# A graph-network stack on one core: layer 2's polynomial at half width, and layer 0's turned adjacency of four groups made for all graphs at once through device memory

## The chip, the cores and the metric

The kernel runs on one core of a Trainium2 chip. Time is the device time in microseconds (us); three runs of the kernel before gave 2142.8, 2142.81 and 2144.53 us, a median of 2142.81 us. The profile is of one further execution.

The engines are called by their names in the profile: PE is TensorE (matmul), PEld its weight loads, DVE is VectorE, ACT is ScalarE, POOL is GpSimd and SP is SyncE, which here only issues transfers (DMAs). "L825" is line 825 of the kernel before.

## What is computed

128 graphs of 64 nodes with 256 features pass through four layers, each followed by a residual addition and a layer norm. All arithmetic is in float32.

```python
# layer 0: five groups of nodes (25, 9, 7, 6 and 6 of the first 25), two graph convolutions each
A = adj[:, idx][:, :, idx] + eye;  deg = A.sum(-1);  dinv = where(deg == 0, 0, deg ** -0.5)
h   = relu((dinv[:, :, None] * A * dinv[:, None, :]) @ (x_g @ W1[g]) + b1[g])
out = relu((same normalized A) @ (h @ W2[g]) + b2[g]);   fused[:, idx] += softmax(fusion_w)[g] * out
# layer 1: one convolution with (adj + eye), normalized in the same way, over all 64 nodes
# layer 2: P = adj / (row_sum + 1e-9);  out = leaky((c0 + c1 P + c2 P^2 + c3 P^3) (x W^T) + b)
# layer 3: five steps of m = h @ weight[l];  agg = (adj != 0)^T m;  h = GRU(agg, h)
```

## The kernel before, in words

**Layer 0** works in 16 units. A unit holds up to four tiles, and a tile as many graphs of one group as fit 128 rows. In order, units 0 to 2 are of group 1, 3 and 4 of group 2, 5 and 6 of group 3, 7 and 8 of group 4, and 9 to 15 of group 0. For unit i, `load0` loads the pieces of the adjacency (`a`, three buffers) and the node rows (`xg`, six buffers); `prep` adds the identity (`ae`, L447), sums rows (`deg`, L453), takes the power -0.5 on POOL (`d0r`, L144), scales the rows, spreads them into a block diagonal matrix (`A0`, L459), turns each tile on PE against an identity (`pT`, L467) and scales the columns on the way out of PSUM (`AT`, L472). Then `aggregate` multiplies node rows by `AT` (`pa`, L484), `hidden` and `support` apply W1 and W2 (`ph` L500, `ps` L516), `add` multiplies by `AT` again (`po`, L538) and adds the result into `F`, the sum over groups. `finish` does the residual and layer norm of the group-0 units. The loop over i runs `load0(i + 3)`, `add(i - 1)`, `aggregate(i + 1)`, `support(i)`, `prep(i + 2)` and `hidden(i + 1)`.

**Layers 1 and 2** are the generator `mid(c)`, for a chunk of eight graphs: four pairs of graphs, 128 rows each. The adjacency `Ab` is block diagonal (128 x 4 x 128). `mid` makes its turned form `AT1` with two DVE block turns (L271, one for each half of the rows), the mask `A01` for layer 3, the row sums, the diagonal `dg` (L290) and the scaled adjacency `An` (L296). `power` computes the polynomial of layer 2 in its turned form by Horner's rule: L302 makes `poly` from `AT1` and `dg`, then twice `pp = An^T poly` on PE (L314, four products of 128 x 128 x 128) and `poly = c_k dg + pp` on DVE (L317). `gather` (L254) and `product` (L325) do the rest on PE. The first two chunks of `mid` run inside layer 0 (from unit 9 on); the others are the filler of layer 3.

**Layer 3** handles two chunks at a time, alternating: ten steps for a pair of chunks, 79 steps in all plus a last one written out. A step's gates are seven products each (`R1` to `R7`, `N1` to `N7`, L825), with copies by ACT (L845), sums by DVE (L849), sigmoid, tanh and updates. The order of all these instructions, on every engine, is one of five strings, `ORDERS`: step numbers 8, 9, 0 and 1 modulo ten have their own, the rest share "p". A letter `p` in a string is one piece of the filler, which is a stretch of `mid` up to its next `yield`, or a piece of a finished chunk's output.

**What sets the order.** PE runs in program order throughout. In layer 3 all engines do. In layer 0 a scheduler orders the other engines ahead of time, and `tc.issue_after(x)` holds a block behind instruction x; once built, each engine's order is fixed. Every transfer that SP issues also waits for the one that SP or ACT issued eight before it on these queues.

Of the kernel before, what the change touches and what calls it, by code (L numbers as in the profile page):

```python
# [9 lines left out]
F32 = mybir.dt.float32  # L10
AF = mybir.ActivationFunctionType
ALU = mybir.AluOpType
AX = mybir.AxisListType
PSUM = bass.MemoryType.PSUM

B, N, D, HID, L = 128, 64, 256, 512, 5
NG, NJ = 5, 25
GROUPS = [
    list(range(25)),
    [0, 1, 2, 3, 4, 5, 6, 7, 8],  # L20
    [0, 9, 10, 11, 12, 13, 14],
    [6, 7, 8, 12, 13, 14],
    [3, 4, 5, 9, 10, 11],
]
# [3 lines left out]
NP = CB // 2  # L28
NE = 15

RUNS = [[(0, 25)], [(0, 9)], [(0, 1), (9, 6)], [(6, 3), (12, 3)], [(3, 3), (9, 3)]]
# [10 lines left out]
class Unit:  # L42
# [23 lines left out]

ORDERS = {
    "p": """
h u4 l u3 R1 r1 t7 R2 p u7 R5 f0 f1 e R6 r6 d0 N1 N2 A2 n1 y B2 p N6 R7 S2 X2
r7 n6 T2 p N5 R4 A7 S7 N7 n7 p B7 R3 S4 U2 N4 A3 S3 d1 X7 N3 B3 X3 X4 G p T4 T3  # L70
""",
    "8": """
h u3 u4 R1 f0 R2 p t7 l u7 r1 R5 f1 R6 N1 d0 n1 p p N2 B2 d1 N6 A2 r6 S2 X2 R7
N5 r7 R4 p A7 n6 N7 y R3 e p n7 B7 N4 A3 S4 S7 T2 X7 N3 S3 B3 X4 G X3 T4 p U2
T3
""",
    "9": """
u3 u4 R1 h R5 t7 u7 R2 r1 A2 f0 d0 R6 p f1 l N1 r6 n1 p N2 B2 S2 R7 X2 d1 p N6
r7 N5 n6 T2 R4 A7 N7 S4 e U2 n7 p R3 y B7 S7 N4 X7 G p N3 A3 S3 B3 X4 X3 T4 T3
""",  # L80
    "0": """
u3 h t7 l R1 u4 u7 R2 R5 r1 R6 f0 f1 N1 A2 r6 n1 N2 N6 R7 S2 y B2 N5 d0 p n6 r7
X2 e T2 N7 A7 p U2 d1 n7 R4 S7 p B7 R3 A3 G p N4 N3 S4 X7 S3 B3 X4 X3 T4 T3
""",
    "1": """
p h u4 R1 R2 t7 l u7 r1 u3 A2 f0 f1 R5 R6 N1 e N2 r6 n1 S2 B2 d0 p N6 n6 R7 N5
r7 A7 y N7 n7 X2 d1 T2 p p R4 B7 R3 N4 S7 U2 X7 S4 A3 N3 B3 S3 X3 G X4 p T4 T3
""",
}

# [2 lines left out]
def gnn_stack(  # L93
# [25 lines left out]
    nc = tc.nc  # L119
# [13 lines left out]
    def spread(src, n, name, pool=wp, eng=None):  # L133

        return const(bass.AP(tensor=src.tensor, offset=src.offset, ap=[[0, 128], [1, n]]), [128, n], name, eng, pool)
# [72 lines left out]
    def psum(name):  # L208
        return pt.tile([128, 512], F32, tag="pt", name=name)
# [50 lines left out]
    state = {}  # L260
    Ab = keep.tile([128, NP, 128], F32, name="Ab")
    AT1 = keep.tile([128, NP, 128], F32, name="AT1")

    def mid(c, first=False):

        aB = adjs.pop(c)
        A01 = keep.tile([128, NP, 128], F32, name="A01", bufs=4)
        with tc.issue_after(evictions[-1].ins) if first else nullcontext():
            for two in range(2):
                b = slice(two * N, (two + 1) * N)  # L270
                nc.vector.transpose(AT1[b, :, b], aB[b])  # L271
        with tc.issue_after(evictions[-1].ins) if first else nullcontext():
            nc.vector.tensor_scalar(A01, Ab, 0.0, None, op0=ALU.not_equal)
        if not first:
# [11 lines left out]
        nc.vector.tensor_scalar(rsum, rsum, 1e-9, None, op0=ALU.add)  # L286
        if not first:
            yield
        dg = keep.tile([128, NP, 128], F32, name="dg", bufs=1)
        nc.vector.tensor_mul(  # L290
            dg, ident[:, None, :].to_broadcast([128, NP, 128]), rsum[:, :, None].to_broadcast([128, NP, 128])
        )
        poly = keep.tile([128, NP, 128], F32, tag="poly", name="poly3", bufs=2)
        nc.scalar.activation(poly, dg, AF.Identity, scale=cw[:, 2:3])
        An = keep.tile([128, NP, 128], F32, name="An", bufs=1)
        nc.vector.tensor_mul(An, Ab, rinv[:, :, None].to_broadcast([128, NP, 128]))  # L296
# [2 lines left out]

        dinv1 = inv_sqrt_end(*root)  # L300
        with tc.high_priority():
            nc.vector.scalar_tensor_tensor(poly, AT1, cw[:, 3:4], poly, op0=ALU.mult, op1=ALU.add)  # L302
        if not first:
            yield
        nc.vector.tensor_add(AT1, AT1, ident[:, None, :].to_broadcast([128, NP, 128]))
        for two in range(2):
            b = slice(two * N, (two + 1) * N)
            nc.vector.tensor_mul(AT1[b, :, b], AT1[b, :, b], dinv1[b, :, None].to_broadcast([N, NP, N]))
        yield

        def power(poly, k):
            p = psum("pp").rearrange("p (q n) -> p q n", q=NP)
            for q in range(NP):
                nc.tensor.matmul(p[:, q, :], An[:, q, :], poly[:, q, :], start=True, stop=True)  # L314
            poly = keep.tile([128, NP, 128], F32, tag="poly", name=f"poly{k}", bufs=2)
            with tc.high_priority():
                nc.vector.scalar_tensor_tensor(poly, dg, cw[:, k : k + 1], p, op0=ALU.mult, op1=ALU.add)  # L317
            return poly

        def product(u, W):  # L320
            p = psum("pd").rearrange("p (q d) -> p q d", q=2)
# [69 lines left out]
    with ExitStack() as c0:  # L391
# [10 lines left out]
        def load0(i, after=None):  # L402

            u = UNITS[i]

            qa = {0: [nc.sync, nc.scalar, nc.gpsimd, nc.sync], 1: [nc.sync, nc.scalar]}.get(i, [nc.sync])
            qx = nc.gpsimd if i < 3 else nc.sync
            a = work.tile([TR, 4, NJ], F32, name="a", bufs=3)
            xg = work.tile([TR, 4, D], F32, name="xg", bufs=6)
            w = u.n if u.g < 2 else NE  # L410
            runs = []
            for t, (b0, nb) in enumerate(u.tiles):
                row = 0
                for f, m in RUNS[u.g]:
                    runs.append((slice(row, row + nb * m), t, slice(b0, b0 + nb), slice(f, f + m)))
                    row += nb * m
            for rows, t, b, f in runs:
                qa[t % len(qa)].dma_start(a[rows, t, :w], adj[b, f, 0:w])

            def nodes():  # L420
                for rows, t, b, f in runs:
                    qx.dma_start(xg[rows, t, :], x[b, f, :])

            if after == "later":
                later[i] = nodes
            else:
                with tc.issue_after(after.ins) if after else nullcontext():
                    nodes()
            loads[i] = a, xg

        def prep(i):
# [38 lines left out]
            for v in scale:  # L470
                with tc.high_priority():
                    evictions.append(nc.vector.tensor_mul(*v))  # L472
            A[i] = AT, xg

        def aggregate(i):
# [147 lines left out]
        def load_first(g):  # L623
            nc.sync.dma_start(W1[:, g], w1[g].rearrange("(k p) e -> p k e", p=128))

        def load_second(g):
            nc.sync.dma_start(W2[:, g], w2[g].rearrange("(k p) e -> p k e", p=128))

        load_first(1)

        def products(l, q):

# [17 lines left out]
        def stage(f, i, first=0):  # L650
            if first <= i < NU:
                f(i)

        g0 = next(i for i, u in enumerate(UNITS) if u.g == 0)
        for i in range(-2, NU + 1):
            if i >= 0:
                stage(load0, i + 3)
            stage(add, i - 1)
            if i:
                stage(aggregate, i + 1)  # L660
# [8 lines left out]
            if i == -1:  # L669

                hidden(0)
                with tc.issue_after(evictions[1].ins):
                    prep(1)
            else:
                stage(prep, i + 2)
                stage(hidden, i + 1)
            if i == -2:
                with tc.issue_after(powers[0].ins):
                    later[1]()
                nc.scalar.dma_start(block0[:, 2:3], c_block0[:, 2:3])  # L680
                load_second(1)
                load0(2, powers[0])
                load_first(2)
            elif i == -1:
                load_second(2)
                load_first(3)
                for ks in (slice(3, 5), slice(0, 1)):
                    nc.sync.dma_start(block0[:, ks], c_block0[:, ks])
            elif i == 0:
                load_second(3)  # L690
            elif i < 5:
                (load_first, load_second)[(i - 1) % 2]((4, 0)[(i - 1) // 2])
            early_stage(i, 2)
# [2 lines left out]
                    if min(o + 1, 9) == j:  # L696
                        f(o)
            if i == 0:

                with tc.issue_after(evictions[-1].ins):  # L700
                    nc.vector.memset(F, 0.0)
                with tc.issue_after(evictions[2].ins):
                    fm = small.tile([128, 1], F32, name="fm")
                    nc.vector.tensor_reduce(fm, fw, AX.X, ALU.max, negate=True)
# [10 lines left out]
                    nc.vector.tensor_mul(gb2, b2c.rearrange("p (g k) -> p g k", k=2), gw[:, :, None].to_broadcast([128, NG, 2]))  # L715
            elif i == 1:
                with tc.issue_after(powers[-1].ins):
                    for t in (Ab, AT1):
                        nc.gpsimd.memset(t, 0.0)
                    cw = spread(conv_w, 4, "cw", eng=nc.gpsimd)  # L720
                    cb = spread(conv_b, 1, "cb", eng=nc.gpsimd)
                    l1bs = spread(l1b, D, "l1bs", eng=nc.gpsimd)
                    L1W = const_later(l1w.rearrange("(k p) e -> p k e", p=128), [128, 2, D], "L1W")
                    L2W = const_later(l2wT.rearrange("(k p) e -> p k e", p=128), [128, 2, D], "L2W")
                    bih = const_later(bihT, [128, 6], "bih")
                    bhh = const_later(bhhT, [128, 6], "bhh")
                    mask = const_later(maskT, [128, B // 2], "mask")
                brz = wp.tile([128, 4], F32, name="brz")
            elif i == 4:
                with tc.issue_after(evictions[5].ins):  # L730
                    nc.vector.tensor_add(brz, bih[:, 0:4], bhh[:, 0:4])

                ih = keep.tile([128, 4, 2, D], F32, tag="RZ", name="ih", bufs=2)
                wl = keep.tile([128, 4, 2, D], F32, tag="RZ", name="wl", bufs=2)
# [544 lines left out]
```

## Time and profile before

| | |
|---|---|
| median of three runs | 2142.81 us (2142.8 to 2144.53) |
| the profiled execution | 2143.39 us; its span, from first to last instruction, 2141.6 us |
| TensorE clock granted | 0.998 |
| layer 0, about | 0 to 300 us of the span |
| ten steps of layer 3 with filler | about 229 us |

The page lists for each engine its busy time, its share of the span and its number of instructions. A group's line has the kernel line, engine, operation, what is written and read, shapes and count; after the bar, busy time and the mean of one in ns; after the next bar, the engine's idle time ahead of it and what ended it. A line of the chain of waits has start, duration, engine, tile, line and count.

### The profile page before, as it was taken

Reading aid. Unit: us, or ns where it says so; the run is one execution under the profiler, and the core shown is the slowest. Engines: PE = TensorE matmul, PEld = TensorE weight load, DVE = VectorE, ACT = ScalarE, POOL = GpSimd, SP = SyncE. Lnnn points to the kernel's source line nnn. Section 1 sums busy time; section 2 is a strip of 40 time slices with the busy share of each in tenths; the row PEclk is TensorE's granted clock in tenths of the full one; section 3 lists DMA queues with packets and bytes.
Section 4 is the critical chain, followed back from the end, with each engine's and each line's share of the span. In section 5 each row is a group of like instructions: output and inputs, shape, how many; then the busy total and the mean of one; then the engine's idle time right before and its main releaser. Section 6 shows DMA issues by size and latency. Waiting matters only on the chain.

```text
span 2141.6 us, 31460 instructions
## 1 busy us (share of the span) xinstructions
PE 2111.7 (99%) x10738; PEld 1817.7 (85%) x10738; DVE 1667.3 (78%) x3849; ACT 979.4 (46%) x2006; POOL 597.3 (28%) x635
## 2 busy tenths in 40 slices
PE   9999999999999999999999999999999999999997
PEld 6777788888888888888888888888888888888886
DVE  3345667777888799788979898889888897888766
ACT  3333344444544455444544454444444454445444
POOL 3411131222323323222323232223232232323222
PEclk9999999999999999999999999999999999999999
DMA  6642110223421253114321342224311521234121
GB/s 166 176 134 64 37 39 21 59 55 66 95 67 40 53 110 76 43 46 87 90 52 42 76 96 63 51 62 85 81 40 47 106 74 40 60 62 96 42 59 40
DMA packets 521995, 149.77 MB, mean 70 GB/s; under 512 B 488702, under 2 KB 516860, under 8 KB 521836
## 3 DMA queue, kind: packets, MB, share of 16 engines
q1 hardware_dynamic: 516996, 142.58, 27.7%
q0 software_dynamic: 2128, 4.77, 0.9%
q8 instruction: 85, 1.39, 0.3%
q10 hardware_dynamic: 2712, 0.42, 0.1%
q14 instruction: 74, 0.61, 0.1%
HBM read 82.67 MB, written 65.01 MB: 69 GB/s over the span
## 4 chain that ended last, share of the span: by engine, by line
PE 78%; DVE 15%; issue 2%; DMA 2%; SPq 1%; ACT 1%; POOL 0%; DVEq 0%; POOLq 0%; ACTq 0%
PE parz L825 20%; PE pdrz L825 10%; PE pan L825 10%; PE pa L254 7%; PE pd L325 5%; PE pdn L825 5%; PE pbrz L825 5%; PE ps L516 5%; PE ph L500 4%; PE pbn L825 2%; DVE RZ L947 2%; DVE NI L983 1%; DVE RZ L946 1%; PE pp L314 1%; DVE NI L984 1%
## 5 line engine op out<-in xcount | busy, mean ns | idle before, releaser
L926 ACT ACTIVATE RZ<-RZ,brz 128x256 f32<-128x256 f32 x474 | 214.8, 501 | 229.3 <-DVE RZ L849 228.9
L825 PE MATMUL parz<-Th,WHH 128*128 128x256 f32 x960 | 290.8, 384 | 6.3 <-ACT c L845 6.2
L805 POOL TENSOR_TENSOR Ta<-agg 128x512 f32<-128x512 f32 x80 | 103.4, 1293 | 681.4 <-ACT agg L256 681.4
L845 ACT COPY c<-parz 128x512 f32<-128x512 f32 x240 | 138.9, 579 | 327.9 <-PE parz L825 327.3
L825 PE MATMUL parz<-Ta,V 128*128 128x256 f32 x960 | 285.5, 379 | 0.0
L825 PEld LDWEIGHTS parz<-Th,WHH 128*128 128x128 f32 x960 | 177.5, 190 | 44.8 <-ACT c L845 22.3
L825 PEld LDWEIGHTS parz<-Ta,V 128*128 128x128 f32 x960 | 182.5, 190 | 24.7
L941 ACT ACTIVATE NI<-NI,bih 128x256 f32<-128x256 f32 x316 | 151.4, 505 | 96.0 <-DVE NI L984 95.9
L845 ACT COPY c<-pan 128x512 f32<-128x512 f32 x237 | 138.1, 583 | 107.1 <-PE pan L825 106.6
L170 POOL TENSOR_TENSOR rs<-ve,mhalf 128x4 f32<-128x4 f32 (+2 forms) x65 | 66.8, 1028 | 400.5 <-DVE ve L163 347.9
L947 DVE TENSOR_TENSOR RZ<-RZ 128x256 f32<-128x256 f32 x316 | 150.4, 476 | 10.7
L805 POOL TENSOR_TENSOR Th<-hn 128x512 f32<-128x512 f32 x64 | 81.6, 1276 | 262.1 <-DVE hn L948 234.6
L849 DVE TENSOR_TENSOR NI<-pdn,c 128x512 f32<-128x512 f32 x158 | 108.3, 685 | 57.6 <-ACT c L845 50.1
L825 PE MATMUL pan<-Ta,V 128*128 128x256 f32 x474 | 144.7, 387 | 0.0
L825 PE MATMUL pan<-Th,WHH 128*128 128x256 f32 x474 | 141.0, 379 | 0.0
L946 DVE TENSOR_TENSOR RZ<-hn,NI 128x256 f32<-128x256 f32 x252 | 119.3, 474 | 23.9 <-ACT NI L941 23.5
L983 DVE SCALAR_TENSOR_TENSOR NI<-NI,bhh,RZ 128x256 f32<-128x256 f32 x237 | 121.0, 511 | 18.8 <-ACT RZ L926 10.0
L849 DVE TENSOR_TENSOR RZ<-pdrz,c 128x512 f32<-128x512 f32 x160 | 109.5, 685 | 27.6 <-ACT c L845 18.0
L254 PEld LDWEIGHTS pa<-A,h 128*128 128x128 f32 x1024 | 124.5, 192 | 7.2 <-issue 3.9
L254 PE MATMUL pa<-A,h 128*128 128x128 f32 x1024 | 125.4, 275 | 3.1 <-DMA h<-hb 2.9
L256 ACT COPY agg<-pa 128x512 f32<-128x512 f32 x160 | 92.0, 582 | 61.3 <-PE pa L254 60.5
L948 DVE TENSOR_TENSOR hn<-RZ,NI 128x256 f32<-128x256 f32 x256 | 111.2, 434 | 9.2
(225 smaller groups left out, 4782.9 us busy)
## 6 DMA issues: line engine op xcount, KB each, us to landing
hb<-flip SPq DMA_DIRECT2D x184, 256.0 KB
h<-hb SPq DMA_DIRECT2D x624, 64.0 KB
out_dram<-xt SPq DMA_DIRECT2D x30, 256.0 KB
hT<-hb SPq DMA_DIRECT2D x112, 64.0 KB
W<-in_w_dram SPq DMA_DIRECT2D x10, 512.0 KB
xt<-xb SPq DMA_DIRECT2D x32, 156.0 KB
xo<-in_x_dram SPq DMA_DIRECT2D x9, 512.0 KB
xb<-xo SPq DMA_DIRECT2D x9, 512.0 KB
```

The lines of the kernel that those rows point to most:

```text
L254: nc.tensor.matmul(p[:, q * 128 : (q + 1) * 128], src(q, k), m[:, q, :], start=True, stop=True)
L325: nc.tensor.matmul(p[:, h, :], ag[:, k, q * 128 : (q + 1) * 128], W[:, k, :], start=k == 0, stop=k == 1)
L805: nc.gpsimd.tensor_sub(t[:, 0:2, :], a[:, :, H:], a[:, 0, :].rearrange("p (s n) -> p s n", s=2))
L825: nc.tensor.matmul(bank[:, g, :], w[:, q, i - 1, :], rhs, start=i in (1, 2, 5) and g == 0 and m == 0, stop=m == len(side) - 1, skip_group_ ...
L845: nc.scalar.copy(c, self.a)
L849: nc.vector.tensor_add(v, self.b if i == 2 else self.d, self.copies.pop({7: 7, 2: 1, 3: 6}[i]))
L926: nc.scalar.activation(v, self.g.a[:, q, :] if i == 4 else v, AF.Sigmoid, bias=brz[:, 2 * q + j : 2 * q + j + 1])
L941: nc.scalar.activation(n, n, AF.Tanh, bias=bih[:, 4 + j : 5 + j])
L946: nc.vector.tensor_sub(d, self.hT[:, j, f], n)
L947: nc.vector.tensor_mul(d, d, z)
L948: nc.vector.tensor_add(self.hn[:, j, f], d, n)
L983: nc.vector.scalar_tensor_tensor(n[:, j, f], h, bhh[:, 4 + j : 5 + j], r[:, j, f], op0=ALU.add, op1=ALU.mult)
```

## The change

1. **Compact polynomial.** The two graphs of a pair sit one above the other, so the turned polynomial can be kept as 128 x 4 x 64 instead of a block diagonal 128 x 4 x 128. One DVE block turn makes `aT` (128 x 4 x 64); `dg`, `poly` and `pp` are 64 columns wide; only the last step writes into a block diagonal `poly0`, in two halves. `An` stays 128 wide.
2. **Layer 0 of groups 2, 3, 4 and 0.** `prep` remains for group 1 (units 0 to 2). For the others the adjacency of all 128 graphs is loaded once (`AL`: 4 x 32 rows, and in a row all 32 graphs of a quarter). `norm_all` adds the identity and takes all four groups' degrees and one power of 128 x 128; `norm_group` scales, turns by a DVE 32 x 32 block turn, scales again and stores the turned normalized adjacency to device memory (`nt`); `load_turned` loads a unit's rows of it, and `spread_out` writes the block diagonal `AT` straight from these rows. The PE transposes of these units go.
3. **Around it.** The zeroing of `F` goes from DVE to POOL; `AL` and `AU` share memory with the weights `ih` and `wl`, which are loaded one unit later (i = 5 instead of 4); `poly0` and a compact identity `eyec` are set up on POOL; all five `ORDERS` strings are rewritten.

```diff
@@ ORDERS, "p" (the others likewise)
-h u4 l u3 R1 r1 t7 R2 p u7 R5 f0 f1 e R6 r6 d0 N1 N2 A2 n1 y B2 p N6 R7 S2 X2
-r7 n6 T2 p N5 R4 A7 S7 N7 n7 p B7 R3 S4 U2 N4 A3 S3 d1 X7 N3 B3 X3 X4 G p T4 T3
+u3 u4 R1 r1 t7 p R2 u7 l R5 h f0 f1 e R6 r6 d0 N1 A2 n1 N2 B2 p S2 N6 R7 X2 r7
+n6 T2 p N5 R4 y A7 U2 N7 S7 n7 p S4 R3 B7 A3 N4 S3 X7 d1 N3 B3 X3 X4 G p T4 T3
@@ mid
-            for two in range(2):
-                b = slice(two * N, (two + 1) * N)
-                nc.vector.transpose(AT1[b, :, b], aB[b])
+            aT = keep.tile([128, NP, N], F32, name="aT", bufs=1)
+            nc.vector.transpose(aT, aB)
...
-            p = psum("pp").rearrange("p (q n) -> p q n", q=NP)
+            p = psum("pp")[:, : NP * N].rearrange("p (q n) -> p q n", q=NP)
             for q in range(NP):
                 nc.tensor.matmul(p[:, q, :], An[:, q, :], poly[:, q, :], start=True, stop=True)
...
+            for two in range(2):
+                b = slice(two * N, (two + 1) * N)
...
+                    nc.vector.scalar_tensor_tensor(
+                        poly0[b, :, b], dg[b], cw[b, 0:1], p[b], op0=ALU.mult, op1=ALU.add
+                    )
+            return poly0
@@ layer 0
+        def norm_all():
+            nc.vector.tensor_add(AL, AL, eye1[:, None, :].to_broadcast([128, 32, 32]))
...
+            nc.vector.tensor_reduce(seg, AL[:, :, 3:15].rearrange("p b (s m) -> p b s m", m=3), AX.X, ALU.add)
...
+            nc.vector.tensor_reduce(deg[:, 0, :], AL[:, :, 0:NJ], AX.X, ALU.add)
+            nc.vector.scalar_tensor_tensor(s, all_deg, 0.0, all_deg, op0=ALU.is_equal, op1=ALU.add)
+            e = mhalf[:, :1].to_broadcast([128, 128])
+            powers.append(nc.gpsimd.tensor_tensor(r, s, e, ALU.pow))
+            o = w0.tile([128, 128], F32, name="roots")
+            nc.vector.scalar_tensor_tensor(o, all_deg, 0.0, r, op0=ALU.not_equal, op1=ALU.mult)
+            return o
+
+        def norm_group(g, dinv):
...
+            S = AS[len(nts) % 2]
+            for f, m in RUNS[g]:
+                nc.vector.tensor_mul(S[:, :, f : f + m], AL[:, :, f : f + m], d.to_broadcast([128, 32, m]))
+            nc.vector.transpose(AU.rearrange("p b n -> p (b n)"), S.rearrange("p b n -> p (b n)"))
...
+                nc.vector.tensor_mul(t[:, :, o : o + m], AU[:, :, f : f + m], d.to_broadcast([128, 32, m]))
...
+                for v in range(4):
+                    nc.sync.dma_start(
+                        nt[32 * v : 32 * v + 32, o : o + m, :].rearrange("b j i -> j b i"),
+                        t[32 * v + f : 32 * v + f + m, :, :n],
+                    )
...
+        def load_turned(i):
...
+                for f, m in RUNS[u.g]:
+                    nc.sync.dma_start(a[row : row + nb * m, t, : u.n], nts[u.g][b0 : b0 + nb, o : o + m, :])
...
+        def spread_out(i):
...
+                        last = nc.vector.tensor_mul(
+                            AT[:r, ts, o : o + nb * m].rearrange("p t (b n) -> p t b n", n=m),
+                            a[:r, ts, None, c : c + m].to_broadcast([r, w, nb, m]),
...
@@ the loop over units
+            if i == 0:
+                with tc.issue_after(evictions[-1].ins):
+                    roots = norm_all()
+            if 0 <= i < 4:
+                norm_group((2, 3, 4, 0)[i], roots)
+            stage(load_turned, i + 3, 3)
+            if i > 0:
+                stage(spread_out, i + 2)
...
-                stage(prep, i + 2)
+                if i <= 0:
+                    prep(i + 2)
...
+                with tc.issue_after(powers[0].ins):
+                    nc.gpsimd.memset(r2, 0.0)
+                    for v in range(4):
+                        b = slice(32 * v, 32 * v + 32)
+                        nc.gpsimd.dma_start(eye1[b], c_ident[b, b])
+                for v in range(4):
+                    b = slice(32 * v, 32 * v + 32)
+                    nc.sync.dma_start(AL[b], adj[b, 0:32, 0:32].rearrange("b i j -> i b j"))
...
+                with tc.issue_after(powers[-1].ins):
+                    nc.gpsimd.memset(F, 0.0)
...
-                with tc.issue_after(evictions[-1].ins):
-                    nc.vector.memset(F, 0.0)
...
-                    for t in (Ab, AT1):
+                    for t in (Ab, AT1, poly0):
                         nc.gpsimd.memset(t, 0.0)
+                    eyec = wp.tile([128, N], F32, name="eyec")
...
+                        nc.gpsimd.dma_start(eyec[b], c_ident[b, b])
...
+            elif i == 5:
...
                 ih = keep.tile([128, 4, 2, D], F32, tag="RZ", name="ih", bufs=2)
```

Built, the changed kernel has this program order where the prediction needs it. On POOL: the memset of `r2` (`AU` and the other scratch, 128 x 2048), four `eye1` transfers, unit 1's power, the memset of `F`, unit 2's two powers, the memsets of `Ab`, `AT1`, `poly0`, two `eyec` transfers, eight constants (`cw` to `mask`), and then the power of 128 x 128. On DVE: `norm_all` up to L494 (its `is_equal`), the `AT` of unit 2, `roots` (L498), the scaling, turn and scaling of group 2 with the first scaling of groups 3 and 4 in between. On SP: two of unit 4's eight node-row transfers, the eight stores of group 2, the eight loads of unit 3, the other six, then the same for group 3 and unit 4, and for group 4 and unit 5 with its node rows ahead.

## The prediction

> **What bounds the kernel now.** I read the page first (busy shares), then the groups by form of TensorE (PE) and GpSimd (POOL), then the chain of waits, then the timelines of 0 to 62 us. The profiled execution took 2143.39 us: a span of 2141.6 us and 1.8 us around it. That is 0.6 us above the median of the runs, 2142.81 us.
>
> ```profile
> PE 2111.7 (99%) x10738; PEld 1817.7 (85%) x10738; DVE 1667.3 (78%) x3849; ACT 979.4 (46%) x2006; POOL 597.3 (28%) x635
> ```
>
> PE is busy for 99% of the span, so only two things move the time: PE work that goes away, and new PE waits. Next, the two kinds of PE record that the change touches:
>
> ```profile
> L314 PE MATMUL pp<-poly,An 128*128 128x128 f32 x256 | 33.7, 275 | 0.0
> ...
> L467 PE MATMUL pT<-ident,A 126*126 126x126 f32 x21 | 3.5, 276 | 0.0
> ```
>
> An fp32 product is two records, each with a weight load of its own (10738 of both). The 275 ns is latency. The pace is in the chain:
>
> ```profile
> 111.86 1.79 PE pa L484 x16
> ...
> 128.08 1.91 PE pa L484 x12
> ```
>
> Sixteen records of 126 columns take 1.79 us, 0.112 us each. Twelve, of which four have only 12 columns, take 1.91 us: narrow records do not save time here.
>
> **The start** matters because PE is in program order. The chain shows when unit 3, the first unit of group 2, is aggregated:
>
> ```profile
> 45.06 0.39 PE pT L467 x4
> 45.45 1.98 PE ph L500 x16
> 47.43 1.78 PE po L538 x16
> 49.21 1.77 PE pa L484 x16
> ```
>
> PE runs back to back there, so lateness of unit 3's turned adjacency beyond about 49 us becomes PE idle time one for one.
>
> **Two rules of the Trainium skill.** (1) "TensorE: Matmul & The Clock Gate", section "LDWEIGHTS (loading the stationary operand)": a weight load takes its number of columns over 1.2 GHz, whatever the rows, so about 107 ns for 128 columns. The trace agrees: in the last unit of layer 0, at 292.9 us, the four records with 75, 75, 125 and 125 columns fill 0.447 us start to start, 112 ns each like full ones, and their weight loads start 110 to 114 ns apart. The forecast goes by the trace. (2) "GPSIMD Engine Reference", section 3.1, puts an elementwise operation at about 2.6 cycles an element at 1.2 GHz, which would make 128 columns 0.3 us. The POOL groups say otherwise for the power operation:
>
> ```profile
> L170 POOL TENSOR_TENSOR rs<-ve,mhalf 128x4 f32<-128x4 f32 x56 | 58.8, 1051 | 328.3 <-DVE ve L163 285.6 <-DVE deg L453 42.6
> ...
> L1037 POOL TENSOR_TENSOR rs<-ve,mhalf 128x2 f32<-128x2 f32 x2 | 1.4, 697 | 7.5 <-DVE ve L1035 7.5
> L144 POOL TENSOR_TENSOR d0r<-d0s,mhalf 12x1 f32<-12x1 f32 x2 | 1.1, 540 | 2.2 <-DVE d0s L142 2.2
> L170 POOL TENSOR_TENSOR rs<-ve,mhalf 128x3 f32<-128x3 f32 x1 | 0.8, 848 | 2.0 <-DVE ve L163 2.0
> ```
>
> One column 540, two 697, three 848, four 1006 (median): 154 ns for each column over 0.39 us, and rows do not matter. The forecast goes by this slope.
>
> **The change, part by part.**
>
> *Compact polynomial.* The moving operand of `pp` falls from 128 to 64 columns, the stationary one (`An`) stays at 128. By rule 1 its 256 records keep 112 ns: saving 0. Bounds: 0, and 256 x 0.053 = 13.7 us if columns counted. I take 0. On DVE each of 16 `mid` calls loses one of two transposes (0.43 us), and about half of `dg` (0.77), of the multiply of L302 (0.93), of L305 (0.69) and of one L317 (0.74), some 2.0 us together, and pays about 0.2 for the second `poly0` write: -1.8 us, 29 us in all. DVE is not the bound, so only what PE waits for it counts. Ten steps (780.8 to 1010.1 us) take 229.3 us; their 840 records of 256 columns at 216 ns and 256 of 128 at 112 ns make 210; with the 64 of L325, 13.8, 223.9. So 5.4 us per ten steps are waits, 2 of them in one step (1133 to 1139 us) where DVE's layer norm and these transposes stand ahead of `RZ<-pdrz`, which PE awaits (0.78 us). I take 0.5 to 0.6 us per ten steps, seven times: -4 us. The five ORDERS strings are rewritten too, with as many pieces of filler per ten steps (50); their effect is unknown, bounded by the waits there are: -12 to +6.
>
> *Removed transposes.* Units 3 to 15 lose `prep`: 48 of the 58 `pT` records at about 0.111 us. The four of unit 3 lie before the point where PE will wait, so 44 count: -4.9 us. DVE's `ae`, `deg`, `A0` groups and POOL's small powers go too; all lay beside PE.
>
> *The new chain for unit 3.* (a) SP: the eight `a` loads give way to four `AL` loads from about 15.9 us; SP issues a transfer every 0.3 to 1.5 us there, each waiting for the one eight before, so they land near 23.5 (`a` loads did at 23 to 25). (b) DVE: `AL` plus identity (1024 columns, 1.2 by L549's 1008), reductions of 384 and 800 (0.55 and 0.95 by L278's 0.68 for 512), four small adds (0.65), L494 (0.28): done near 27.2. (c) POOL: ahead of the new power stand, in program order, the memset of `AU` and four `eye1` transfers (4.2 us from 10.7; unit 1's root slides from 11.1 to about 15, its `A0` is ready at 17.3, and PE wants it at 18.4: hidden, with 1 us of cover), the F memset moved from DVE (3840 columns, 3.5 us by L719's 0.55 for 512, done as unit 2's root arrives at 20.3), then behind that root (21.4) three memsets (1.4), two `eyec` transfers (1.1) and the eight constants:
>
> ```profile
> 33.97 0.55 POOL L719 MEMSET Ab<- 128x512 f32 x1
> 34.43 0.55 POOL L719 MEMSET AT<- 128x512 f32 x1
> 34.90 0.63 POOL L130 DMA_DIRECT2D cw<-in_conv_w_dram  x1
> ...
> 39.15 0.54 POOL L130 DMA_DIRECT2D mask<-in_maskT_dram  x1
> ```
>
> These eight take 4.8 us, so the power starts at about 28.7 us. (d) The power: 0.39 + 128 x 0.154 = 20.1 us, until 48.8. Bounds: 0.6 us if the columns are pipelined (0.39 plus a share of L805's 1.29 us for 512), 20.1 by the slope; I take the slope. (e) DVE waits for it at L498 with the scaling and turning queued behind: 0.28 + 0.17 + 0.35 + 0.25 + a 32x32-block turn of 1024 columns (2 x 0.69) + 0.25 + 0.17 + 0.35, done at 52.1. (f) SP: eight `nt2` stores, then eight loads of `a` from `nt2`. The view of SP's queue gives the pace:
>
> ```profile
> 35.70 4.92 SPq L422 DMA_DIRECT2D xg<-in_x_dram  x8
> ```
>
> 0.6 us each (0.45 for `h<-hb`), and 1.7 us to land: 52.1 + 4.5 + 4.5 + 1.7 + about 0.7 for loads that await their store = 63.5. (g) `spread_out` on DVE (0.23 + 0.55 by L459) and a semaphore: 64.3. PE's `pa` of unit 3 moves from 49.05 to 64.3: **+15.3 us**.
>
> *Behind that wait.* SP stands before the `nt2` stores with unit 4's node rows, `nt3` and unit 4's loads behind: 6 + 8 + 8 more issues at 0.45 to 0.6 give 73 to 76, landed and spread by 75 to 77, and PE wants them 12.9 us after unit 3, at 77.2. Just in time: +0.5 (0 to 2). Unit 5 (27 issues more) has about 1.5 us of cover, later units over 8. The 28 stores and four `AL` loads are 32 more SP issues, some 17 us of a queue that is full until 110 us; this is why units 4 and 5 are tight. `ih` and `wl`, loaded one unit later, are needed at 300 us: hidden.
>
> *Clock.* PE idle for 15 us is likely to lose its full clock: the kernel starts at half (eight records of 512 columns in 6.78 us, 0.85 us each, against 0.42 later), and reaches full pace about 6.5 us after its first matmul. The page of rule 1, "Part 1: The HAM clock gate", says that an idle window of about 3.4 us halves the clock until a busy one has passed. Half of 3.4 to 6.5 us is 1.7 to 3.3: I estimate +2.5 (0 to 3.5); no stall of this length in the trace of before shows it.
>
> *Sum:* +15.3 + 0.5 + 2.5 - 4.9 - 4 + 0 = +9.4; 2143.39 + 9.4 = 2152.8 as profiled, 0.6 less for the median: **2152 us**.
>
> **Rivals.**
>
> - *The power is short* (faster). If 128 columns cost no more than about 4.5 us, the chain ends at 28.7 + 4.5 + 15.5 = 48.7 and PE never waits: -5.3 - 4 = -9.3, 2133.5 us. POOL may overlap columns in long rows (L805: 2.5 ns a column for a subtraction); against it, the slope is straight from one column to four. At 10 us, the waits and the savings would cancel.
> - *The compact product counts*: weight loads do not bind, -13.7 on top of the forecast, 2138.5. The 75-column records speak against it.
> - *The orders gain much*: half or more of the 5.4 us per ten steps vanishes, -15 instead of -4: 2141. Lighter DVE work speaks for it; most of these waits are short ones behind ACT copies, which the change does not shorten.
> - *The change does nothing that counts*: on PE the polynomial part is that already.
>
> **How the numbers follow.** Forecast (a PE stall of 12 to 18 us) 0.69; power short or half as long 0.17; compact product 0.07; orders 0.07. A measurement here tells 0.2%, 4.3 us, from no change. The forecast alone spans 2145 to 2160 and is slower by more than that in nine cases of ten; the rival of the short power is mostly faster; the two others straddle no change. Together: faster 0.19, same 0.17, slower 0.64. The range takes in the straddling rivals and half of the short power: 2136 to 2160.
>
> **What would show it.** A POOL power of 128x128 at 20 us from about 29 us; DVE `roots` waiting for it until about 49; a PE gap ahead of `pa` of unit 3 of some 15 us and PEclk below full just after; `pp` with 256 records still 0.111 us apart; ten steps in 228 to 229 us. Wrong if the power lasts under 5 us, if PE does not wait before 60 us, or if ten steps fall to 226.

## The result, and the profile after

The changed kernel takes 2160.74 us (median of six runs, 2159.89 to 2163.05), the kernel before 2143.19 beside it: a ratio of 1.0081, 95% interval 1.0068 to 1.0094. It is slower by about 17.5 us, where 9.4 were forecast. The profiled execution takes 2161.12 us, its span 2158.9 us.

The first line of the page, engine by engine (busy us, share of the span, instructions):

```profile
PE 2109.2 (98%) x10690; PEld 1821.2 (84%) x10690; DVE 1636.5 (76%) x3771; ACT 977.7 (45%) x2006; POOL 605.9 (28%) x629
```

PE has 48 records less, the removed transposes. It is busy for 2.5 us less, in a span that is 17.3 us longer, so it stands still for some 20 us more. The chain of waits says where (start, us, what):

```profile
47.48 1.80 PE po L616 x16
49.28 17.23 issue
66.51 3.73 PE pa L562 x16
...
128.97 1.80 PE po L616 x16
130.76 4.88 issue
135.64 3.75 PE pa L562 x16
```

An `issue` piece is time in which PE stands still and the profile names nothing that it waits for. There are two such stalls: 17.2 us ahead of unit 3 and 4.9 us ahead of unit 7. Behind each, `pa` takes 3.73 and 3.75 us for sixteen records of at most 126 columns, which took 1.77 and 1.79 in the chain before. The windows of those stretches show the clock:

```profile
core 0: us, PE busy (x) PEld busy (x) DVE busy (x) ACT busy (x) POOL busy (x), PEclk, DMA share, GB/s
52.40:72.90 20.50, 6.39 (x23) 5.88 (x24) 12.46 (x34) 1.06 (x2) 1.11 (x2) 0.50 0.12 20
134.30:141.10 6.80, 5.46 (x21) 5.13 (x22) 5.06 (x19) 1.16 (x2) 1.04 (x1) 0.50 0.75 262
```

Half clock (0.50) begins 3.1 and 3.5 us into the stalls and lasts 6.4 and 5.5 us past PE's restart. The chain ahead of unit 3, from the timeline (start, us, engine, line, and in brackets the idle time ahead and what ended it):

```profile
28.00 1.23 DVE L484 TENSOR_TENSOR AL<-AL,eye 128x1024 f32<-128x1024 f32 x1 [4.56 <-DMA AL<-in_adj_dram]
...
31.74 20.76 POOL L496 TENSOR_TENSOR AL<-AL,mhalf 128x128 f32<-128x128 f32 x1 [2.81 <-DVE AL L494]
...
52.53 0.29 DVE L498 SCALAR_TENSOR_TENSOR roots<-AL 128x128 f32<-128x128 f32 x1 [20.61 <-POOL AL L496]
...
55.26 4.18 SPq L517 DMA_DIRECT2D nt<-AU  x8
59.55 4.68 SPq L530 DMA_DIRECT2D a<-nt  x8
...
65.72 0.69 DVE L543 TENSOR_TENSOR AT<-a,block 112x64 f32<-112x64 f32 x2 [1.80 <-DMA a<-nt]
```

POOL waits 2.8 us for the degrees, the power takes 20.8 us, DVE waits 20.6 us for it, and SP, whose queue stands behind the `nt2` stores, issues nothing from 34.0 to 55.3. The last line is `spread_out` of unit 3: it waits for the loads, and PE goes on at 66.51 us, as soon as it is done. The same line of unit 7 shows what that stall waits for; SP's queue ahead of it follows with number 5:

```profile
134.78 0.75 DVE L543 TENSOR_TENSOR AT<-a,block 126x252 f32<-126x252 f32 x2 [7.78 <-DMA a<-nt]
```

The compact product's group, by form, answers to the one shown of before:

```profile
L314 PE MATMUL pp<-poly,An 128*128 128x64 f32 x256 | 32.2, 269 | 0.0
```

From the start times of its records: the first of each block of eight is followed after 56 ns (109 before), the others after 111 to 112 as before. So the record behind the block starts 838 ns after the block's first, 53 ns sooner than before (891). But the start after that one comes 271 ns later instead of 218. What the first record gives is taken back behind the block.

The starts of the 79 steps of layer 3 and of the units' `pa` give the rest of the account:

```
                                    before    after    shift
pa of unit 3                         49.05     66.51   +17.5
pa of unit 4                         62.32     82.60   +20.3
pa of unit 7                        111.70    135.64   +23.9
pa of unit 8                        128.01    154.20   +26.2
first step of layer 3               325.88    348.62   +22.7
last numbered step of layer 3      2086.13   2102.54   +16.4
span                               2141.6    2158.9    +17.3
```

### The profile page after: what moved, and what is told of

Same layout as the page of the kernel before. It is cut to its first block, busy times and chain, and to the rows that moved or that the text cites. A ratio compares the mean times of both kernels' runs of the same rounds, so it can differ in the third digit from the quotient of the medians.

```text
span 2158.9 us, 31300 instructions
## 1 busy us (share of the span) xinstructions
PE 2109.2 (98%) x10690; PEld 1821.2 (84%) x10690; DVE 1636.5 (76%) x3771; ACT 977.7 (45%) x2006; POOL 605.9 (28%) x629
## 4 chain that ended last, share of the span: by engine, by line
PE 88%; DVE 8%; issue 2%; DMA 1%; SPq 0%; ACT 0%; POOL 0%; DVEq 0%; POOLq 0%
PE parz L930 23%; PE pan L930 11%; PE pdrz L930 11%; PE pa L254 8%; PE pbrz L930 6%; PE pdn L930 5%; PE pd L333 5%; PE ps L594 5%; PE ph L578 4%; PE pbn L930 3%; PE pa L562 1%; PE pp L314 1%; PE po L616 1%; PE pf L719 1%; DVE xt L185 1%
## 5 line engine op out<-in xcount | busy, mean ns | idle before, releaser
L1052 DVE TENSOR_TENSOR RZ<-RZ 128x256 f32<-128x256 f32 x316 | 160.0, 507 | 10.8
```

Source lines behind the costliest of these rows:

```text
L1052: nc.vector.tensor_mul(d, d, z)
```

## The experiments

Ten variants were run. A ratio compares a variant with runs of the kernel before on the same chip. There the kernel before took 2145.15 to 2146.16 us, 2 to 3 us more than beside the changed kernel (2143.19), while the expectations start from the lower time; so sizes are better read from the ratios and the traces than from the totals.

**1. Without the power.**

```diff
-            powers.append(nc.gpsimd.tensor_tensor(r, s, e, ALU.pow))
+            powers.append(nc.gpsimd.tensor_tensor(r, s, e, ALU.mult))
```

> The changed kernel with GpSimd's power of 128 columns replaced by a multiplication of the same shape (under 1.5 us for 20.8): the inverse roots of layer 0 are left out, everything else keeps its place. Theory (the power's length sets both stalls: SP is held 21 us by it, and is still late at unit 7): PE reaches `pa` of unit 3 at about 49.5 us without a gap, the gap of 5.1 us at unit 7 shrinks below 1 us, no stretch at half clock; 2160.7 - 17.3 - 3.3 - 5.1 - 2.7 = about 2132 us. Rival 1 (unit 7's gap comes from nt0's slow stores and POOL's transfers at that place): the first gap goes, the second stays, 2140 us. Rival 2 (the way through device memory, 16 issues and two landings, is late by itself): unit 3 still waits over 5 us, 2146 us or more.

Measured: 2140.39 us, ratio 0.998 (0.9973 to 0.9986). The instruction takes 0.40 us, and in the chain of waits unit 3 is on time, but the second stall is still there:

```profile
108.28 1.80 PE po L616 x16
110.08 5.16 issue
115.24 3.75 PE pa L562 x16
```

Rival 1 holds. The power explains the first stall with its clock loss, about 20 us (a ratio of 0.998 for 1.0081). Unit 7's stall keeps its size (5.2 us for 4.9) though SP now goes on 20 us earlier (35.0 for 55.3): it moves with the chain. Rival 1 names two causes, the stores and POOL's transfers; number 5 moves the stores and leaves POOL's transfers where they are.

**2. Four powers of 32 columns.**

```diff
+            for v in (1, 2, 3, 0):
+                powers.append(nc.gpsimd.tensor_tensor(o[v], s[:, 32 * v : 32 * v + 32], e, ALU.pow))
...
+            nc.vector.scalar_tensor_tensor(o[v], c, 0.0, o[v], op0=ALU.not_equal, op1=ALU.mult)
```

> The changed kernel with the power cut into four of 32 columns, that of group 2 first, and each group's correction for degree zero made only ahead of its own scaling (the degrees in tiles of their own). Theory (154 to 160 ns for each column, and unit 3 needs 32 of the 128): each piece 5.3 to 5.5 us, the first done near 37 us; 16 issues of SP, two landings and the spreading put `pa` of unit 3 at 51 to 52 us, a gap of 2 to 3 us[...]: 2160.7 - 15 - 3.3 = 2142 with unit 7's gap as it was, 2134.5 without it. Rival (the four powers keep DVE and SP waiting one after another as before, since DVE is in order): unit 3 still at 60 us or later, 2155 us.

Measured: 2156.32 us, ratio 1.005 (1.0036 to 1.0063). The timeline of DVE shows why:

```profile
36.68 0.23 DVE L506 SCALAR_TENSOR_TENSOR roots<-deg,roots 128x32 f32<-128x32 f32 x1 [5.30 <-POOL roots L498]
42.08 0.23 DVE L506 SCALAR_TENSOR_TENSOR roots<-deg,roots 128x32 f32<-128x32 f32 x1 [5.17 <-POOL roots L498]
47.46 0.22 DVE L506 SCALAR_TENSOR_TENSOR roots<-deg,roots 128x32 f32<-128x32 f32 x1 [5.16 <-POOL roots L498]
47.61 0.64 DVE L510 TENSOR_TENSOR AU<-AL,roots 128x32 f32<-128x32 f32 x3
```

A piece takes 5.4 us, as the columns say. But the scheduler had put the corrections (L506) of groups 3 and 4 ahead of group 2's scaling (L510), so DVE waited for three powers, and PE ahead of unit 3 for 12.3 us. The rival's mechanism is what happened, with its time.

**3. Layer 0's part alone, and 4. the polynomial and the strings alone.** Number 3 keeps the new layer 0 and takes `mid` and `ORDERS` from the kernel before; number 4 is the reverse. Of 4:

```diff
-h u4 l u3 R1 r1 t7 R2 p u7 R5 f0 f1 e R6 r6 d0 N1 N2 A2 n1 y B2 p N6 R7 S2 X2
+u3 u4 R1 r1 t7 p R2 u7 l R5 h f0 f1 e R6 r6 d0 N1 A2 n1 N2 B2 p S2 N6 R7 X2 r7
...
-            p = psum("pp").rearrange("p (q n) -> p q n", q=NP)
+            p = psum("pp")[:, : NP * N].rearrange("p (q n) -> p q n", q=NP)
```

> The new layer 0 with the polynomial and the five order strings of the kernel before. Theory (the whole loss is in layer 0, the compact polynomial has no part in it): layer 3 begins 22 to 25 us later than before and its ten steps take 228 to 229.3 us, 2143.2 + 22.7 = 2166 us. Rival (the second stall came from the early polynomial work on DVE, POOL's extra memset and two `eyec` transfers): no gap at unit 7, 2158 us.

> The kernel before with the compact polynomial and the new order strings, its own layer 0. Theory (layer 3's gain of 6.2 us comes from these two and does not need the rest): layer 0 ends within 1 us of before, the steps 0 to 78 shrink by 5 to 7 us, 2137 us. Rival (the gain in layer 3 was only lateness taken up by waits that were there already, since layer 3 began 23 us later): 2143 us.

Measured: number 3, 2172.14 us, ratio 1.0122 (1.0108 to 1.0136); number 4, 2135.81 us, ratio 0.9952 (0.9939 to 0.9964). The two ratios multiply to 1.0073, near the whole change's 1.0081. In number 3, PE stops for 18.0 us ahead of unit 3 and 2.9 ahead of unit 7, layer 3 begins at 347.5 us, and its steps take 1762.2 us (1760.2 before): the loss is layer 0's. In number 4, layer 3 begins at 325.8 us and its steps take 1751.4 us, so the gain needs nothing of the new layer 0. Both theories hold in their direction, and both effects are larger than expected. Number 3 is 6 us above its 2166; its profiled execution was the fastest of four (2167.58 us, clock 0.992), the others had a clock of 0.989 to 0.990, and where they lost it no trace shows. Number 4's steps shrink by 8.8 us, where 5 to 7 were expected; traces with the same layer 3 differ by some us (see numbers 7 and 8).

**5. Group 0 scaled and stored two turns later.**

```diff
-            if 0 <= i < 4:
-                norm_group((2, 3, 4, 0)[i], roots)
+            if i in (0, 1, 2, 5):
+                norm_group({0: 2, 1: 3, 2: 4, 5: 0}[i], roots)
```

> The changed kernel with group 0's scaling, turning and its four stores made at unit 5's turn instead of unit 3's, ahead of unit 9's loads, the first that read them. Theory (SP issues without a pause from 36 or 55 us on, 0.74 us and more for each transfer, and nt0's four stores and the load behind them hold it for 9 to 10 us at the worst place): unit 7's loads are issued 9 to 10 us earlier, its gap of 5.1 us and the 2.7 us of half clock behind it go, unit 3's gap of 17.4 us stays; 2160.7 - 7.8 = 2153 us. Rival (the stores hold SP as long wherever they stand, and unit 9 or 10 waits instead): a gap of 4 us or more later in layer 0, 2160 us.

Measured: 2153.87 us, ratio 1.0053 (1.0039 to 1.0067). SP's queue of the changed kernel ahead of unit 7:

```profile
101.49 7.39 SPq L517 DMA_DIRECT2D nt<-AU  x4
108.92 6.18 SPq L530 DMA_DIRECT2D a<-nt  x6
...
126.93 6.15 SPq L530 DMA_DIRECT2D a<-nt  x8
```

and of this run:

```profile
101.13 4.52 SPq L530 DMA_DIRECT2D a<-nt  x6
...
113.89 6.15 SPq L530 DMA_DIRECT2D a<-nt  x8
```

Unit 7's eight loads (the x8 lines) are issued 13 us earlier: 7.4 us are the stores, and the rest is mostly the load right behind them (2.4 us instead of 0.8) and SP's waits for earlier transfers, which this run does not have there. The chain of waits of this run has no `issue` piece there any more:

```profile
128.35 1.78 PE po L616 x16
130.14 1.79 PE pa L562 x16
```

Unit 7 starts 5.7 us earlier than in the changed kernel, unit 8 8.4 us earlier. The theory holds. DVE's work for group 0 moved along with the stores, but ahead of unit 7 DVE had been waiting for the loads (7.8 us, the line of L543 shown with the result), so it is the stores' place that decides. The stores take nearly as long where they now stand (6.47 us for four, from 128.6), but there SP has time to spare.

**6. The roots by ScalarE and VectorE.**

```diff
-            powers.append(nc.gpsimd.tensor_tensor(r, s, e, ALU.pow))
+            nc.scalar.activation(r, s, AF.Sqrt)
+            powers.append(nc.vector.reciprocal(r, r))
```

together with the edit of number 5.

> The changed kernel with the roots of layer 0 made by ScalarE (square root of 128 columns) and DVE (reciprocal) in place of GpSimd's power, and nt0 made at unit 5's turn as in the run before. Theory: the roots are there 1.5 to 3 us after the degrees, near 34 us, unit 3 is aggregated at 49 to 50 us without a gap, no gap at unit 7, no half clock; the first run without the power gave 2140.4 with unit 7's gap and its clock loss, 7.9 us together, so 2132 to 2133 us, faster than both kernels. Rival (ScalarE waits for the degrees until 31.7 us ahead of unit 1's four `relu`, and loads a function table twice): PE waits 2 to 5 us for `hg` of unit 1, 2135 to 2138 us.

Measured: 2132.45 us, ratio 0.995 (0.9938 to 0.9963), faster than both kernels. Timeline of ACT and DVE:

```profile
28.42 1.28 ACT L496 ACT_TABLE_LOAD   x1
30.85 0.31 ACT L496 ACTIVATE AL<-AL 128x128 f32<-128x128 f32 x1 [1.15 <-DVE AL L494]
...
31.20 0.95 DVE L497 RECIPROCAL AL<-AL 128x128 f32<-128x128 f32 x1
32.18 0.29 DVE L499 SCALAR_TENSOR_TENSOR roots<-AL 128x128 f32<-128x128 f32 x1
```

The root is there 1.3 us after the degrees instead of 20.8. Unit 3's `AT` is spread from 46.6 us, PE reaches its `pa` at 48.71 us without a stall, and layer 3 begins at 319.9 us, 6.0 us earlier than before. ACT's table load falls into a pause, and its four `relu` of unit 1 are not late enough for PE to see.

**7. The compact polynomial alone, and 8. the order strings alone.** The edits are the two halves of number 4's diff.

> The kernel before with the compact polynomial alone, old order strings. Theory (the product's 64 columns give PE nothing, DVE's 29 us less are mostly hidden): the 256 `pp` records keep their pace, layer 3 (step 0 to step 78) 1756 to 1759 us for 1760.2 before, 2140 to 2142 us. Rival (the lighter DVE work is the whole gain and the strings only go with it): layer 3 at 1752 to 1754, 2136 us.

> The kernel before with the new order strings alone, old polynomial. Theory (half the gain of layer 3 is the strings'): step 0 to step 78 1755 to 1758 us, 2138 to 2141 us. Rival (the strings are fitted to the lighter polynomial and do nothing, or harm, without it): 1760 us or more, 2143 us or more.

Measured: number 7, 2140.07 us, ratio 0.9975 (0.9967 to 0.9982); number 8, 2141.58 us, ratio 0.9986 (0.9978 to 0.9995). The steps of layer 3 take 1756.7 us with the polynomial alone (-3.5), 1757.2 with the strings alone (-3.0). Both theories hold, number 8 0.6 us above its range. By the ratios both halves gain something, and the two together (0.9952) gain more than either. The steps' totals can't say how much is whose: the eight traces that have the changed kernel's layer 3 (the changed kernel, numbers 1, 2, 4, 5, 6, 9 and 10) take from 1751.4 to 1756.1 us for it. The `pp` records of number 7 start in the pattern of the changed kernel (838 ns, then 272), so fewer columns give PE nothing by themselves. Where each half acts is seen in the steps: of the first ten, step 8 has 3.2 us beyond its records' pace before, 3.55 with the polynomial, 0.34 with the strings; step 4 has 1.07 before, 0.26 with the polynomial, 1.06 with the strings. The first ten steps take 227.0 us before, 226.5 with the polynomial, 224.4 with the strings and 223.6 in all eight traces with both: there the split is clear, and most of it is the strings'.

**9. Four powers, each group behind its own.** As number 2, but each correction is held behind the scaling of the group before it, and `nt0` is late as in number 5.

```diff
+            with tc.issue_after(scaled[-1].ins) if scaled else nullcontext():
                 nc.vector.scalar_tensor_tensor(o[v], c, 0.0, o[v], op0=ALU.not_equal, op1=ALU.mult)
```

> The four powers of 32 columns again, now with each group's correction kept behind the scaling of the group before it, so that group 2 waits for its own power alone; nt0 at unit 5's turn. Theory (about 0.165 us for each column, 5.4 us a piece, and 14.4 us from roots to spread as with ScalarE's root): roots at 36.7 us, spread at 51.1, `pa` of unit 3 at about 52, a gap of 3 us with no or little half clock behind it; 2132.5 + 3 = 2135.5 us. Rival (SP's queue or the stores hold it up too, beyond the power): a gap of 6 us or more, 2139 us or more.

Measured: 2140.78 us, ratio 0.9976 (0.9965 to 0.9988). The first root is there at 36.9 us and SP has issued unit 3's last load by 48.5, as expected. Then the timeline of DVE shows:

```profile
50.86 0.43 DVE L516 TENSOR_TENSOR AU<-AL,roots 128x96 f32<-128x96 f32 x2
53.12 0.19 DVE L507 SCALAR_TENSOR_TENSOR roots<-deg,roots 128x32 f32<-128x32 f32 x1 [1.82 <-POOL roots L498]
53.49 0.69 DVE L548 TENSOR_TENSOR AT<-a,block 112x64 f32<-112x64 f32 x2 [0.18 <-DMA nt<-AU]
```

Group 0's correction (L507) stands ahead of unit 3's spreading (L548), and DVE waits for the fourth power until 53.1 us. PE stops for 5.3 us and loses another 2 to the clock. Neither theory was right: the time is the rival's, but the cause is the power again, not SP: the fourth power keeps DVE for 1.8 of the 2.3 us that the stall exceeds the forecast.

**10. PE kept busy in the stall.**

```diff
+            if i == 1:
+                p = psum0("pw")
+                for _ in range(18):
+                    nc.tensor.matmul(p, zero[:, :128], zero, start=True, stop=True)
```

> The changed kernel with 18 products of the zero tile (fp32, 512 columns, nothing reads them) put on PE ahead of unit 3's aggregation, 15.3 us at full clock, inside the gap of 17.4 us. Theory (the idle time itself takes the clock away, and the time lost behind it is the clock's): the remaining gap is about 2 us, no stretch at half clock behind unit 3, 3.3 us less: 2157.4 us, unit 7 as before. Rival (PE is slow behind the gap because its operands or its queue are late): the records behind unit 3 stay at twice their pace, 2160.7 us or more.

Measured: 2166.36 us, ratio 1.0098 (1.0082 to 1.0114), a miss in the total. The timeline of PE shows the products (L750), which stand ahead of unit 2's `pa` (52.14), and unit 3 behind its stall:

```profile
34.91 15.61 PE L750 MATMUL pw<-zero 128*128 128x512 f32 x36
...
66.48 2.01 PE L562 MATMUL pa<-AT,xg 112*128 112x112 f32 x16 [2.04 <-issue]
68.32 3.74 PE L594 MATMUL ps<-W,hg 128*126 128x256 f32 x16
```

The window of 52.4 to 72.9 us has a clock of 1.00 (the third figure from the end) where the changed kernel had 0.50:

```profile
52.40:72.90 20.50, 18.46 (x107) 15.17 (x106) 9.66 (x30) 8.28 (x17) 1.01 (x1) 1.00 0.12 20
```

From unit 3's `pa` to unit 4's, PE needs 13.0 us; the changed kernel needs 16.1, number 6 without a stall 12.9. So the clock cost 3.1 us there, as the theory said, and these 2 us of idle PE cost none. But none of it reached the end: PE waited more ahead of units 5 and 6 (1.2 and 0.8 us), and unit 7 started at 136.6 us instead of 135.6. The chain of waits, which in this run follows SP's queue, names what held it:

```profile
102.23 1.83 SPq L517
104.11 2.29 SPq L517
106.44 2.39 SPq L517
108.88 2.42 SPq L530
...
130.65 5.97 issue
136.62 3.75 PE pa L562 x16
```

Three of `nt0`'s four stores and the load behind them take 9 us of the queue. The unit's start is SP's, not PE's: the same finding as number 5's from the other side. The remaining 6 us of the miss come at 329.8 us, where PE stands still for 3.1 us and loses its clock again; in no other run is there a PE gap there. PE waits for DVE, which has waited 3.1 us for a load of `WHH`, until 331.7 us. That load is not late in itself: in the changed kernel DVE waits 3.5 us for it, until 331.9 us, and PE goes on meanwhile. What ties PE to it here stays open; the added PE work takes a turn of the PSUM buffers and may have shifted those behind it.

## Why the prediction was wrong

The direction and the mechanism of the first stall were right, from the power to PE. The sum was too small by 8 us, and nearly all of that is a second stall which the forecast had ruled out: 4.9 us ahead of unit 7, and 2.7 us at the clock behind it. Against its steps:

- **(a), AL's landing: wrong by 4.5 us.** `AL` was to be there at 23.5 us, DVE started on it at 28.0. The forecast had taken over the issue times of the `a` loads it replaces. In the changed kernel SP waited 4.7 us ahead of them for an earlier transfer (`b`; 0.6 us before), and one of the four issues alone took 3.4 us. POOL's own queue (c) was free at 28.9 us as worked out (28.7), so the power began 3.0 us late, at 31.7.
- **(d), the power: right.** 20.76 us for 20.1 by the slope. Columns in an access of 128 get no cheaper: 162 ns each. The bound of 0.6 us did not come near; a multiplication of the same shape takes 0.40 us (number 1).
- **(e) to (g): right.** From `roots` to `pa`, 14.0 us for 15.5. Unit 3 came at 66.5 for 64.3: +17.5 instead of +15.3.
- **"Behind that wait": the step that failed.** Units 4 and 5 were just in time as forecast, but "later units over 8" (us of cover) was wrong: unit 7 waited 4.9 us. The mis-sized term is SP's queue ahead of unit 7's loads. `nt0`'s four stores, each with a 25-element piece for each of 800 row-and-graph pairs, were costed as ordinary issues of 0.45 to 0.6 us; three of them and the load behind them take 8.8 us, and with SP's waits behind them they make unit 7's loads 13 us later (number 5). Where they are moved away, unit 7 is spread at 122.4 us, 7.5 us before PE asks for it, near the cover of the forecast. The pace of the other issues was too short as well, but alone it leaves that cover. It had been read from transfers of 96 and 16 rows (units 3 and 4); those of units 5 to 8 have 63 rows and take 0.73 to 0.8 us, and the kernel before shows this too:

```profile
42.60 6.53 SPq L418 DMA_DIRECT2D a<-in_adj_dram  x8
...
75.35 6.30 SPq L422 DMA_DIRECT2D xg<-in_x_dram  x8
```

In the changed kernel SP made 94 issues from 55.3 to 126.9 us, 60.9 us of issuing in 71.6, and could not catch up. That it is SP and these stores is shown by numbers 5 (moved: the wait is gone) and 10 (PE is 3 us earlier at unit 4, and unit 7 is no earlier); that it does not come from the long power, by number 1.
- **Clock: right for one stall, and missed for the second.** 3.1 us behind unit 3 (2.5 forecast, 0 to 3.5; measured by number 10). Behind unit 7, 2.7 us that the forecast lacks with its stall: from unit 7's `pa` to unit 8's, 18.6 us against 15.8 in number 5.
- **Transposes: right.** Where nothing else differs, a unit is shorter by 0.44 us, four times 0.111; 11 units make 4.9.
- **Layer 3: -6.3 instead of -4, differently spread.** The six windows of ten steps behind the first give 0.5 us each on average (228.7 to 228.3), as was taken. The wait of 0.8 us in each ten steps that the forecast had named, PE for `RZ<-pdrz`, is gone. The first ten steps give 3.4 us (227.0 to 223.6), of which the strings alone give 2.6. Their effect had been called unknown and left out of the sum, so this part of the gain was luck; without it the sum would have missed by more.
- **Compact product: right.** Nothing, in all runs with it. The page "TensorE: Matmul & The Clock Gate", section "LDWEIGHTS (loading the stationary operand)", had been taken for it: the time of a weight load goes by its number of columns, 128 here, and the forecast took this load to pace the record whatever moves. The trace agrees: from the second of a block on, the weight loads start 110 to 113 ns apart with 64 moving columns as with 128. The 56 ns after a block's first record show that a narrow record alone can be shorter, and the 271 ns behind the block that this gains nothing while the loads keep their pace. The four records that the prediction cites at 292.9 us are 112 ns apart only on average; their starts are 69, 112, 154 and 112 ns apart, the same pattern.

The account by starts: +17.5 to unit 3, +2.8 to unit 4 (clock, less transposes), -1.0 to unit 6, +4.6 to unit 7, +2.3 to unit 8 (clock again), -3.5 to the first step, together +22.7; then -6.3 to the last numbered step and +0.9 behind it: +17.3 of span. Of the 8 us that the forecast lacked, 7.6 are unit 7's stall and its clock, 2.2 the later start of unit 3 and 0.6 more clock behind it; layer 3 gave 2.3 more than forecast, and the small rest is spread.

Of the rivals, the short power did not happen, and its 2133.5 us would have been missed by unit 7's stall, 2140.4 in number 1; with the stores moved too it is 2132.45 in number 6. The orders gained less than that rival asked for. As to what would show it wrong, no single sign did: the windows of ten from the second on stayed within 227.5 to 229.2 (only the first fell to 223.6), and PE waited where it should. The missing sign was a second PE gap.

## What to carry to other kernels

When a part is rebuilt so that all units share one chain, cost the chain once for its latency and a second time as a load on the queue that carries it: add up every issue with its own measured duration, up to the last unit, take that duration from a transfer of the same form, and give a store of many small pieces its own row. An operation whose cost rises by column (here the power) is worth moving to an engine where the same shape is short before it is made wide; and a chain that makes one group first only helps if no wait for the other groups is put ahead of that group's next step on any engine.

## What was not expected of the hardware

- GpSimd's power costs 162 ns a column up to 128 columns, while its multiplication of the same 128 x 128 takes 0.40 us in all; ScalarE's square root takes 0.31 and VectorE's reciprocal 0.95.
- A PE stall of 17.2 us and one of 4.9 us cost nearly the same at the clock, 3.1 and 2.7 us, and number 9's of 5.3 us some 2. Each is about half of the time from PE's restart to the return of the full clock (6.4, 5.5 and 4.0 us), in which PE works at half pace. The length of these three stalls does not enter.
- A much shorter stall can cost the clock, too. Near the end of layer 3, PE stands still for 2.16 us in the changed kernel (from 2126.4 us) and keeps its clock; in number 4 the same stall (2101.0 to 2103.2 us) is followed by half clock from 2103.3 to 2106.7. In every trace the changes of the clock lie whole multiples of 3.41 us apart, so it may be the place of a stall in these steps that decides; no run tests this, and in number 3 the clock halves from 118.6 to 122.0 us behind no PE gap of over 0.4 us, which stays open. The page named above, "Part 1: The HAM clock gate", speaks of an idle window of about 3.4 us: the steps agree with it, but the stall of 2.16 us shows that a stall need not fill one.
- An issue on SP goes by the form of the transfer, not by its time in the kernel: the loads `a<-nt` and `xg` of 96 rows take 0.56 and 0.58 us (medians), those of 63 rows 0.73 and 0.75; `xg` in the kernel before has 0.57 and 0.74. Of `nt0`'s four stores of 800 pieces the first takes 0.36 us; the other three take 1.7 to 2.4, and so does the load behind them (2.4 for 0.73). Much of the price of many pieces is paid by what is issued next. Why was not tried.
